# One set of PSUM banks for a small attention, and its last projections moved between the first scores

## The chip, the cores and the metric

The kernel runs on one core of a Trainium2 chip. A core has TensorE (PE in the profile; its weight loads are listed apart as PEld), VectorE (DVE), ScalarE (ACT), GpSimd (POOL) and SyncE (SP), which issues the transfers. Each engine works through its own list of instructions in order and waits on semaphores for the others. Matmul results land in PSUM, which has eight banks of 128 x 512 fp32 values. The metric is the device time of one launch in microseconds, as the median of several runs.

## The reference

The model is a stack of transformer-like blocks on a state `x` of 2 sequences of 256 tokens with 256 features, with a context of 2 x 4096 tokens read by the cross attentions. Each block adds its result to `x`:

```
x = x + L0_xattn(layernorm(x), ctx)      x = x + L0_attn(layernorm(x))   x = x + L0_ffn(layernorm(x))
x = x + L1_xattn(layernorm(x), ctx)      x = x + L1_attn(layernorm(x))   x = x + L1_ffn(layernorm(x))
x = x + L2_xattn(ctx, layernorm(x))      x = x + L2_attn(layernorm(x))   x = x + L2_ffn(layernorm(x))
x = x + L3_xattn(layernorm(x), ctx)      x = x + L3_attn(layernorm(x))   x = x + L3_ffn(layernorm(x))
```

The change concerns two of them, the self attentions of the tokens with 16 heads of 16 features:

```python
def _L1_attn_ref(x, Wq, Wk, Wv, Wu, bu):          # x is the normalized state, 2 x 256 x 256
    q = (einsum('btk,ok->bto', x, Wq) / 4).reshape(b, t, 16, 16)
    kk = (einsum('btk,ok->bto', x, Wk) / 4).reshape(b, t, 16, 16)
    v = einsum('btk,ok->bto', x, Wv).reshape(b, t, 16, 16)
    att = softmax(einsum('bthd,bshd->bhts', q, kk), axis=-1)
    out = einsum('bhts,bshd->bthd', att, v).reshape(b, t, k)
    return einsum('btk,ok->bto', out, Wu) + bu
```

`L3_attn` is the same with one matrix for queries, keys and values, with biases on all of them and on the output, a scale of 1/16, and a band mask: a query sees keys that are at most 128 positions away.

## The kernel before

All blocks are written out one after the other in one program. The state is kept transposed, features on partitions: `x` is 128 x 2 x 512 (two halves of the features, 512 tokens of both sequences). For the two attentions, `small_attention` (L1358) fixes the order of TensorE, VectorE and ScalarE as the program writes it; GpSimd and SyncE are ordered by a scheduler. Before it, the weights are requested by `net.load` in a ring of three buffers.

PSUM is given out by `net.banks`: tiles of one bank in two rings (`mm`, `acc`), and tiles of a pair of banks (128 x 2 x 512) in a ring `sc`. A tile waits until the readers of the tile that had its place before are done. `net.stage` (L97) opens a set with two of each ring, and an SBUF pool `temp` for the pieces of a layer norm.

`small_attention` has three sections.

*Projections*, in a stage of their own. `center` (L223) subtracts the mean of the features and squares (L234, L235). `project` (L1395) then makes, for each of four chunks `c` of 128 padded feature rows (four heads of 32 rows, 16 used), keys and queries of all 512 tokens in one pair of banks `kq_ps`: 2 x 2 matmuls of 128 x 512, each of them two instructions in fp32. After chunk 0, `measure` (L251, L252) has the reciprocal deviation of each token, after chunk 1 `widened` (L271) spreads it over partitions. Then come the values of both pairs of token tiles (`v_ps`, in an `mm` bank), evicted by ScalarE in L1 (L1419) and by VectorE with the bias in L3 (L1422). Then `take` evicts a chunk: VectorE multiplies keys (L1400) and queries (L1404, one per sequence) by the deviation and adds the query bias in L3 (L1406), ScalarE adds the key bias (L1401). With two pairs of banks, chunk 2 reuses the pair of chunk 0, and chunk 3 that of chunk 1.

*Attention*, with another set of banks: `mm` 1, `sc` 3, `acc` 1. There are eight units (sequence, chunk), each with four heads. For a unit, `first_scores` forms the scores of 256 x 256 of four heads in two pairs of banks, by 16 instructions on 32 rows each (L1469), in L3 followed by four bf16 matmuls that add the band (L1477); VectorE takes the negated maximum of each row (L1494, two reductions). `shift_queries` transposes these maxima (L1505) and adds them to the queries as one more feature (L1506), so that the second scores, `scores`, come out shifted and transposed; ScalarE takes their exponential (L1513). `weigh` multiplies with the values (L1524), `inverses` and `normalize` divide. The loop in `attend` runs these staggered: round i transposes the maxima of unit i-1, forms the first scores of unit i, weighs unit i-3, normalizes unit i-4 and forms the second scores of unit i-1. Two scores and two pairs each are four `sc` tiles per round on three pairs of banks, so a tile reuses the place of the third before it.

*Output projection*, in a stage again (`add_projection`, L316).

Of the kernel before, what the change touches and what calls it, by code (L numbers as in the profile page):

```python
# [30 lines left out]
NT = T // P  # L31
# [8 lines left out]
NC16 = H * HP // P  # L40
# [30 lines left out]
class Net:  # L71
# [229 lines left out]
    def project(self, w, chunks, m):  # L301

        ps = self.mm("proj")
        self.matmuls(ps, [(w[:, d, m * P : (m + 1) * P], c) for d, c in enumerate(chunks)])
        return ps
# [294 lines left out]
def run(steps, n=None):  # L600

    for _ in steps if n is None else zip(range(n), steps):
        pass
# [188 lines left out]
class ContextAttention:  # L792
# [46 lines left out]
    def take_queries(self, norm, wq, q_bias, alive):  # L839

        net, nc = self.net, self.nc
        by_batch = lambda ap: ap.rearrange("p (b s) -> p b s", b=NB)
        self.q_bias, self.alive = q_bias, alive
        pair = net.sc("q_ps")
        chunks = net.mm("q_ps"), net.mm("q_ps"), pair[:, 0], pair[:, 1]

        def project(c, copied=True):
            net.matmuls(chunks[c], [(wq[:, d, c * P : (c + 1) * P], of) for d, of in enumerate(norm.chunks)])
            if copied:
                nc.scalar.copy(self.queries[:, :, c], by_batch(chunks[c]))  # L850

        project(0, copied=False)
        net.measure(norm)
        project(1)
        project(2)
        ps = net.widen(norm.rstd)
        nc.scalar.copy(self.wide, ps)
        project(3)
        nc.vector.tensor_tensor(self.q[0], chunks[0][:, :S], self.wide[:, :S], ALU.mult)
        self.add_bias(nc.vector, 0, 0)  # L860
        nc.scalar.copy(self.queries[:, 1, 0], chunks[0][:, S:])
# [145 lines left out]
    def attend(self, vpool, ppool, fpool):  # L1007
        net, nc, PER, LAG = self.net, self.nc, self.PER, self.LAG
        focus = net.focus
        self.vpool, self.ppool = vpool, ppool  # L1010
        for _ in range(4):
            self.load_values_ctx()
        focus.start(self.layer, fpool)
        fills = self.plan()
        n = len(self.UNITS)

        ready = net.sm(1, name="ready", tag="ready")
        nc.scalar.activation(ready, net.eps5, AF.Exp)
        rankings = {}
        for g in range((n + 1) * PER + LAG + 2):  # L1020
            second = g - PER - LAG
            if g < n * PER:
                self.first_scores(g // PER, g % PER)
            run(self.beginning)
            if 1 <= g < n:
                self.finish_queries(g)
            if self.layer == 0:
                for t in self.key_tiles[4:][3 * g : 3 * g + 3]:
                    nc.gpsimd.memset(t, 1.0)
            run(fills.get(g, ()))  # L1030
            for kc in self.rankings.get(g, ()):
                if kc not in rankings:
                    y, _, factor = focus.chunks[kc]
                    rankings[kc] = focus.sparsify(fpool, y, factor)
                run(rankings[kc], 1)
            if 0 <= second < n * PER:
                self.scores(second // PER, second % PER)
            focus.magnitudes_of_taken()
            if 0 <= second - 1 < n * PER:
                self.weigh((second - 1) // PER, (second - 1) % PER)  # L1040
            if g in self.done:
                self.inverses = net.inverses(self.weighed)
                if self.done[g] == n - 1:
                    run(self.normalize(n - 1))
            for kc in self.weighings.get(g, ()):
                run(focus.weighing[kc], 1)
# [311 lines left out]
def small_attention(net, x, wq, wk, wv, wo, scale, qb=None, kb=None, vb=None, ob=None, window=None):  # L1358

    by_program = {mybir.EngineType.PE, mybir.EngineType.DVE, mybir.EngineType.Activation}  # L1360
    with net.tc.manual_schedule(engines=by_program):
        with net.tc.tile_pool(name="sa", bufs=1, reuse_waits="tile") as big, net.tc.tile_pool(name="sa_w", bufs=1, reuse_waits="tile") as work:
            a = SmallAttention(net, big, work, scale, vb, window)
            with net.stage():
                a.project(net.center(net.halves(x)), wq, wk, wv, qb, kb)
            with net.banks(mm=1, sc=3, acc=1):
                a.attend()
            with net.stage():
                return net.add_projection(x, wo, [a.oT[:, c, :] for c in range(NC16)], bias=ob)


class SmallAttention:
# [22 lines left out]
    def project(self, norm, wq, wk, wv, q_bias, k_bias):  # L1395
        net, nc, hc = self.net, self.nc, norm.chunks

        def take(c, k, q):
            of = self.k[:, c, :]
            nc.vector.tensor_tensor(of, k, wide, ALU.mult)  # L1400
            nc.scalar.activation(of, of, AF.Identity, bias=k_bias[:, c : c + 1])  # L1401
            for b in range(NB):
                of, at = self.q[b * NC16 + c], slice(b * S, (b + 1) * S)
                nc.vector.tensor_tensor(of, q[:, at], wide[:, at], ALU.mult)  # L1404
                if q_bias is not None:
                    nc.vector.tensor_scalar_add(of, of, q_bias[:, c : c + 1])  # L1406

        heads = self.v[:, :, : H * VH].rearrange("p t (h e) -> p t h e", e=VH)[:, :, :, :DH]

        def values(t2):  # L1410
            ps = net.mm("v_ps")
            for t in range(2):
                at = slice((t2 + t) * P, (t2 + t + 1) * P)
                net.matmuls(ps[:, t * D : (t + 1) * D], [(c[:, at], wv[:, d, :]) for d, c in enumerate(hc)])
            of = ps.rearrange("p (t h e) -> p t h e", t=2, e=DH)
            for t in range(2):
                rstd = norm.rstd[:, t2 + t : t2 + t + 1]
                if self.v_bias is None:
                    nc.scalar.mul(heads[:, t2 + t], of[:, t], rstd)  # L1419
                else:  # L1420
                    bias = self.v_bias.rearrange("p (h e) -> p h e", e=DH)
                    nc.vector.scalar_tensor_tensor(heads[:, t2 + t], of[:, t], rstd, bias, ALU.mult, ALU.add)  # L1422

        made = []
        for c in range(NC16):
            sc = net.sc("kq_ps")
            for i, w in enumerate((wk, wq)):
                net.matmuls(sc[:, i, :], [(w[:, d, c * P : (c + 1) * P], of) for d, of in enumerate(hc)])
            made.append((c, sc[:, 0, :], sc[:, 1, :]))
            if c == 0:  # L1430
                net.measure(norm)
                continue
            if c == 1:
                wide = net.widened(norm.rstd)
                for t2 in range(0, NT, 2):
                    values(t2)
            for of in made:
                take(*of)
            made = []

    def attend(self):


        n = len(self.UNITS)
        for i in range(n + 4):
            aux = self.net.mm("aux") if 0 <= i - 1 else None
            if 0 <= i - 1 < n:
                self.shift_queries(i - 1, aux[:, S:])
            if i < n:
                self.first_scores(i)  # L1450
            if 0 <= i - 3 < n:
                self.weigh(i - 3)
            if 0 <= i - 4 < n:
                self.normalize(i - 4, aux[:, :S])
            if 0 <= i - 1 < n:
                self.scores(i - 1)
            if 0 <= i - 3 < n:
                self.inverses = self.net.inverses(self.weighed[i - 3], self.acc[:, S:])
# [83 lines left out]
def l1_attn(net, x):  # L1542
    wq, wk = net.load("L1a_wq", "L1a_wk")
    wv, wo = net.load("L1a_wv", "L1a_wo")
    ob, kb = net.vec("L1a_ob"), net.vec("row16")
    return small_attention(net, x, wq, wk, wv, wo, 1.0 / 16.0, kb=kb, ob=ob)
# [446 lines left out]
def l3_attn(net, x):  # L1993
    nc = net.nc
    wq, wk = net.load("L3a_wq", "L3a_wk")
    wv, wo = net.load("L3a_wv", "L3a_wo")
    qb, kb, vb, ob = (net.vec(f"L3a_{n}b") for n in "qkvo")
    return small_attention(
        net, x, wq, wk, wv, wo, D**-0.5, qb=qb, kb=kb, vb=vb, ob=ob, window=P
    )  # L2000
# [363 lines left out]
```

## Time and profile before

| | us |
|---|---|
| median of 3 runs | 2494.8 (2491.27 to 2495.66) |
| profiled execution | 2496.69 |
| its span | 2494.6 |
| L1 attention, first mean matmul after `x` to the next block's | 1611.86 to 1693.72 |
| its projections, first to last chunk | 1614.71 to 1634.84 |
| L3 attention, the same | 2128.87 to 2228.42 |
| its projections | 2132.97 to 2159.45 |
| TensorE busy over the span | 2332.9 |
| VectorE busy | 1532.3 |
| ScalarE busy | 1099.7 |

Times in the profile are microseconds from the start of the span, unless ns is named. A row of the timeline gives start, duration, engine, line, operation, output and inputs, shapes and how many instructions are merged in it; in brackets stands the idle time before it and what ended it. A row of the windows gives the busy time and the number of instructions of each engine in one stretch, then the clock that TensorE was granted as a share of its full speed, the busy share of the transfer engines and GB/s. Line numbers are those of the kernel before.

### The profile page before, as it was taken

Reading aid. Unit: us, or ns where it says so; the run is one execution under the profiler, and the core shown is the slowest. Engines: PE = TensorE matmul, PEld = TensorE weight load, DVE = VectorE, ACT = ScalarE, POOL = GpSimd, SP = SyncE. Lnnn points to the kernel's source line nnn. Section 1 sums busy time; section 2 is a strip of 40 time slices with the busy share of each in tenths; the row PEclk is TensorE's granted clock in tenths of the full one; section 3 lists DMA queues with packets and bytes.
Section 4 is the critical chain, followed back from the end, with each engine's and each line's share of the span. In section 5 each row is a group of like instructions: output and inputs, shape, how many; then the busy total and the mean of one; then the engine's idle time right before and its main releaser. Section 6 shows DMA issues by size and latency. Waiting matters only on the chain.

```text
span 2494.6 us, 42805 instructions
## 1 busy us (share of the span) xinstructions
PE 2332.9 (94%) x17142; PEld 1253.6 (50%) x17142; DVE 1532.3 (61%) x2691; ACT 1099.7 (44%) x1929; POOL 348.2 (14%) x529
## 2 busy tenths in 40 slices
PE   7999999999999699999999999999999986899998
PEld 3454555544544364554454544554448453455453
DVE  4877888788736657877878778443331354334353
ACT  3356555555615334555555565531131352123232
POOL 4000001000024603000010000000011131003020
PEclk9999999999989799999999999989999997788989
DMA  6432233132010124332232231201223100000100
GB/s 196 144 96 91 86 94 92 52 112 65 10 38 35 48 94 127 94 94 87 90 95 86 75 100 29 84 14 51 97 93 93 42 18 14 34 21 12 58 12 22
DMA packets 97798, 174.42 MB, mean 70 GB/s; under 512 B 15120, under 2 KB 63888, under 8 KB 96704
## 3 DMA queue, kind: packets, MB, share of 16 engines
q1 hardware_dynamic: 97600, 171.68, 21.8%
q8 instruction: 136, 2.23, 0.4%
q14 instruction: 62, 0.51, 0.1%
HBM read 154.25 MB, written 0.59 MB: 62 GB/s over the span
## 4 chain that ended last, share of the span: by engine, by line
PE 56%; DVE 5%; ACT 3%; POOL 1%; issue 1%; DMA 0%; ACTq 0%; SPq 0%; DVEq 0%; POOLq 0%
PE s L1149 6%; PE s L1173 5%; PE proj L181 5%; PE attn_acc L1197 5%; PE v_ps L181 4%; PE expert L181 2%; PE k_ps L1070 2%; PE s L181 2%; PE c_acc L1792 2%; PE s L1469 2%; PE ffn_ps L181 2%; DVE mx L1157 2%; PE kq_ps L181 1%; PE f_ps L181 1%; PE kc_sum L181 1%; PE qk_ps L181 1%
## 5 line engine op out<-in xcount | busy, mean ns | idle before, releaser
L1157 DVE TENSOR_REDUCE mx<-s 128x2 f32<-128x1024 f32 x512 | 603.0, 1220 | 229.3 <-PE s L1149 226.6
L1183 ACT ACTIVATE p<-s 128x1024 f32<-128x1024 f32 x512 | 496.0, 1021 | 255.4 <-PE s L1173 253.4
L1173 PE MATMUL s<-xa_q,xa_k 32*128 32x256 f32 x4096 | 342.5, 403 | 25.9 <-DVE mx L1157 23.0
L1149 PE MATMUL s<-xa_k,xa_q 32*128 32x512 f32 x2048 | 337.5, 641 | 5.3 <-ACT p L1183 2.3
L1173 PEld LDWEIGHTS s<-xa_q,xa_k 32*128 32x128 f32 x4096 | 212.8, 184 | 167.7 <-issue 92.6
L1197 PE MATMUL attn_acc<-p,xv 128*32 128x256 f32 x4096 | 276.1, 386 | 0.7 <-ACT p L1183 0.7
L679 DVE TENSOR_TENSOR ge<-fy 128x960 bf16<-128x960 f32 (+14 forms) x240 | 169.5, 706 | 6.5
L1197 PEld LDWEIGHTS attn_acc<-p,xv 128*32 128x32 f32 x4096 | 107.4, 109 | 131.4 <-issue 84.3
L1149 PEld LDWEIGHTS s<-xa_k,xa_q 32*128 32x128 f32 x2048 | 111.3, 183 | 122.6 <-issue 57.5
L633 POOL TENSOR_TENSOR fy<-fy,low 128x256 f32<-128x256 f32 x64 | 46.5, 726 | 866.5 <-ACT fy L632 866.5
L681 DVE TENSOR_TENSOR rank<-rank,ge 128x960 bf16<-128x960 bf16 (+14 forms) x240 | 104.1, 434 | 6.0
L683 DVE TENSOR_TENSOR rank<-rank,ge 128x960 bf16<-128x960 bf16 (+14 forms) x240 | 100.7, 419 | 2.6
L389 POOL TENSOR_SCALAR p<-p,r 128x128 f32<-128x128 f32 (+1 forms) x192 | 83.1, 446 | 128.5 <-DVE r L385 74.5
L1117 ACT COPY xv<-v_ps 128x512 f32<-128x512 f32 x64 | 37.6, 588 | 127.3 <-PE v_ps L181 124.8
L370 ACT ACTIVATE p<-p,top 128x256 f32<-128x256 f32 (+1 forms) x128 | 57.1, 447 | 69.6 <-DVE top L358 68.6
L1070 PE MATMUL k_ps<-ctx_k,w_L0x_wk 128*64 128x512 f32 x256 | 66.8, 616 | 5.3 <-DMA ctx_k<-in_ctxT 5.0
L181 PE MATMUL f_ps<-f_wk,f_ctx 128*128 128x256 f32 x256 | 68.9, 400 | 1.8 <-DMA f_ctx<-in_ctxT 1.8
L181 PEld LDWEIGHTS f_ps<-f_wk,f_ctx 128*128 128x128 f32 x256 | 44.4, 189 | 44.5 <-issue 26.5
L181 PE MATMUL v_ps<-w_L0x_wv,ctx_v 128*128 128x256 f32 x256 | 65.6, 400 | 0.8 <-ACT k_dense L1083 0.8
L1792 PE MATMUL c_acc<-pT,ctx_n 128*128 128x256 f32 x256 | 62.1, 387 | 4.2 <-ACT pT L1765 3.0
L181 PE MATMUL kc_sum<-f_tok,fy 128*128 128x257 f32 x256 | 64.2, 393 | 0.0
L181 PE MATMUL v_ps<-w_L1x_wv,ctx_v 128*128 128x256 f32 x256 | 63.8, 392 | 0.0
(489 smaller groups left out, 3375.7 us busy)
## 6 DMA issues: line engine op xcount, KB each, us to landing
ctx_k<-in_ctxT SPq DMA_DIRECT2D x128, 512.0 KB
ctx_v<-in_ctxT SPq DMA_DIRECT2D x64, 256.0 KB
xa_k<-k_dense SPq DMA_DIRECT2D x512, 32.0 KB
f_ctx<-in_ctxT SPq DMA_DIRECT2D x32, 256.0 KB
f_tok<-in_ctx SPq DMA_DIRECT2D x16, 512.0 KB
ctxT<-in_ctxT SPq DMA_DIRECT2D x16, 512.0 KB
ctx_n<-in_ctx SPq DMA_DIRECT2D x16, 512.0 KB
xa_k<-key_masks SPq DMA_DIRECT2D x128, 8.0 KB
```

The lines of the kernel that those rows point to most:

```text
L181: self.nc.tensor.matmul(out, lhsT=lhsT, rhs=rhs, start=i == 0, stop=i == len(pairs) - 1)
L389: nc.gpsimd.tensor_scalar(p[:, j, :nk], p[:, j, :nk], r[:, j : j + 1], 1.0, ALU.mult, ALU.mult)
L679: nc.vector.tensor_tensor(ge[:, :, :n], w[:, :, :n], w[:, :, P - n :], ALU.is_ge)
L681: nc.vector.tensor_tensor(rank[:, :, P - n :], rank[:, :, P - n :], ge[:, :, :n], ALU.add)
L683: nc.vector.tensor_tensor(rank[:, :, :n], rank[:, :, :n], ge[:, :, :n], ALU.subtract)
L1070: nc.tensor.matmul(ps[i * HR : (i + 1) * HR, :], lhsT=self.wk[:, d, c * HR : (c + 1) * HR], rhs=ctx[:, d, :], start=d == 0, stop=d == ND - 1,)
L1149: nc.tensor.matmul(pairs[i // 2][:, i % 2, :], lhsT=self.q[u][rows, qt * P : (qt + 1) * P], rhs=k[rows, :], start=True, stop=True,)
L1157: nc.vector.tensor_reduce(mx[:, qt, 2 * i : 2 * i + 2, kc], sc, AX.X, ALU.max)
L1173: nc.tensor.matmul(pairs[i // 2][:, i % 2, kk * S : (kk + 1) * S], lhsT=k[rows, at], rhs=self.q[u][rows, :], start=True, stop=True,)
L1183: nc.scalar.activation(p, sc, AF.Exp, scale=DH**-0.5)
L1197: nc.tensor.matmul(self.acc[i * HP : (i + 1) * HP, :S], lhsT=v[:, 2 * k2 + kk, at : at + HP], rhs=ps[i // 2][:, i % 2, kk * S : (kk + 1) * S],
L1792: nc.tensor.matmul(accs[m], lhsT=of[:, (k + i) % (KC // P), m * P : (m + 1) * P], rhs=pT[:, i, :], start=k + i == 0, stop=k + i == KT - 1,)
```

## The change

The projections and the attention share one set of banks (`mm` 1, `sc` 3, `acc` 1), and the `temp` pool stays open through both. `project` becomes a generator, which `attend` drives: its first part makes chunks 0 and 1, the first half of the values, takes chunks 0 and 1, makes chunk 2, the second half of the values, and takes chunk 2; its second part, products and take of chunk 3, runs in the loop right after the first scores of unit 0. No operation is added or dropped. The loop over all values after chunk 1 is split into its two halves, so on ScalarE (L1) and VectorE (L3) the eviction of the second half now stands behind the takes of chunks 0 and 1. On TensorE the order is: chunk 0, variance, chunk 1, widening, values (first half), chunk 2, values (second half), scores of unit 0, chunk 3, transposes of unit 0, scores of unit 1, and so on. On VectorE: take 0, take 1, take 2, reductions of unit 0, take 3, shift of unit 0, reductions of unit 1.

```diff
-            with net.stage():
-                a.project(net.center(net.halves(x)), wq, wk, wv, qb, kb)
-            with net.banks(mm=1, sc=3, acc=1):
-                a.attend()
+            with net.banks(mm=1, sc=3, acc=1), net.tc.tile_pool(name="temp", bufs=2, reuse_waits="tile") as net.temp:
+                a.attend(a.project(net.center(net.halves(x)), wq, wk, wv, qb, kb))
...
-        made = []
-        for c in range(NC16):
+        def products(c):
             sc = net.sc("kq_ps")
             for i, w in enumerate((wk, wq)):
                 net.matmuls(sc[:, i, :], [(w[:, d, c * P : (c + 1) * P], of) for d, of in enumerate(hc)])
-            made.append((c, sc[:, 0, :], sc[:, 1, :]))
-            if c == 0:
-                net.measure(norm)
-                continue
-            if c == 1:
-                wide = net.widened(norm.rstd)
-                for t2 in range(0, NT, 2):
-                    values(t2)
-            for of in made:
-                take(*of)
-            made = []
+            return c, sc[:, 0, :], sc[:, 1, :]
+
+        made = [products(0)]
+        net.measure(norm)
+        made.append(products(1))
+        wide = net.widened(norm.rstd)
+        values(0)
+        take(*made[0])
+        take(*made[1])
+        made = products(2)
+        values(2)
+        take(*made)
+        yield
+        take(*products(3))
+        yield
 
-    def attend(self):
+    def attend(self, projections):
         n = len(self.UNITS)
+        next(projections)
         for i in range(n + 4):
...
             if i < n:
                 self.first_scores(i)
+            next(projections, None)
             if 0 <= i - 3 < n:
                 self.weigh(i - 3)
```

## The prediction

> **What bounds the kernel now.** I read the page first (TensorE 94% busy, 56% of the chain that ended last), then the chain of waits around the two attentions, the timeline of their first 45 us, and last the busy time and granted clock in windows of 3.41 us, because the clock changes only on a grid of that step. The profiled execution took 2496.69 us with a span of 2494.6 us, so 2.1 us lie around the span. The sum is made against it and the forecast is set from the median, 2494.8 us, which is 1.9 us lower.
>
> The timeline of the L1 attention (start, duration, engine, line, operation, idle time before it and what ended that):
>
> ```profile
> 1624.36 3.62 PE L181 MATMUL v_ps<-w_L1a_wv,xc 128*128 128x256 f32 x16
> 1627.81 7.03 PE L181 MATMUL kq_ps<-xc,w_L1a_wq 128*128 128x512 f32 x16
> 1636.38 1.13 PE L1469 MATMUL s<-sa_k,sa_q 32*128 32x256 f32 x12 [0.91 <-DVE sa_q L1404]
> 1637.22 2.36 DVE L1494 TENSOR_REDUCE sa_top<-s 128x4 f32<-128x1024 f32 x2 [0.99 <-PE s L1469]
> 1639.72 0.66 PE L1505 MATMUL aux<-ident,sa_top 128*128 128x128 f32 x2 [2.21 <-DVE sa_top L1494]
> 1645.79 0.69 PE L1505 MATMUL aux<-ident,sa_top 128*128 128x128 f32 x2
> ```
>
> TensorE is fed through the projections (two chunks in 7.03 us, 3.52 each), then waits 0.91 us for VectorE to free a bank pair and 2.21 us for the maxima of the first unit. The first transposes (L1505) open round 1; rounds 2, 3 and 4 open at 1645.79, 1651.82 and 1657.85. Later rounds take 4.8 us. The same places in the L3 attention:
>
> ```profile
> 2147.98 0.88 DVE L1422 SCALAR_TENSOR_TENSOR sa_v<-v_ps,rstd,vectors 128x256 f32<-128x256 f32 x2 [0.85 <-PE v_ps L181]
> 2150.65 8.80 PE L181 MATMUL kq_ps<-xc,w_L3a_wq 128*128 128x512 f32 x16 [2.71 <-DVE sa_q L1404]
> 2165.37 0.66 PE L1505 MATMUL aux<-ident,sa_top 128*128 128x128 f32 x2 [2.32 <-DVE sa_top L1494]
> 2172.61 1.28 ACT L1513 ACT_TABLE_LOAD   x1 [11.67 <-PE s L1477]
> 2172.74 0.64 PE L1505 MATMUL aux<-ident,sa_top 128*128 128x128 f32 x2
> ```
>
> Here chunk 2 starts 2.71 us late, because VectorE evicts all values before it takes chunk 0, and the two chunks take 8.80 us instead of 7.03. Rounds 2, 3 and 4 open at 2172.74, 2181.74 and 2188.45. Windows (length, busy time of PE, PEld, DVE, ACT, POOL with instruction counts, granted clock, DMA):
>
> ```profile
> 1635.74:1639.15 3.41, 1.13 (x12) 0.76 (x12) 2.42 (x4) 1.87 (x2) 0.00 (x0) 1.00 0.74 229
> 1639.15:1642.57 3.42, 2.85 (x20) 2.19 (x22) 0.91 (x3) 0.00 (x0) 0.00 (x0) 0.50 0.01 2
> 1652.81:1656.22 3.41, 3.41 (x32) 1.44 (x28) 1.81 (x3) 0.24 (x1) 0.00 (x0) 0.50 0.00 0
> 2147.73:2151.14 3.41, 0.70 (x2) 0.30 (x2) 3.09 (x8) 0.72 (x1) 0.00 (x0) 1.00 0.00 0
> 2157.97:2161.38 3.41, 2.12 (x10) 0.72 (x8) 2.04 (x6) 0.72 (x1) 0.00 (x0) 1.00 0.23 62
> 2161.38:2164.79 3.41, 1.67 (x16) 1.03 (x16) 2.16 (x3) 0.00 (x0) 0.00 (x0) 1.00 0.62 245
> ```
>
> After a thin window (1.13, 0.70 or 1.67 us busy) the clock is 0.50. In L1 it stays there from 1639.15 to 1656.2, until the weighing of values (L1524) joins; in L3 from 2164.8 to 2185.3. A round then takes 6.03 us in L1.
>
> **The change, L1.** Removed: nothing that computes. Moved: chunk 3 (8 instructions, 3.52 us) goes behind the first score group, and half of the values behind chunk 2. With three bank pairs chunk 2 no longer waits for a bank. TensorE's chain from 1624.36: values 1.81 (half of 3.62), chunk 2 3.52, values 1.81, scores 1.15 (the full-clock groups of 16 at 1661.06), chunk 3 3.52: 1636.17. The first unit's reductions (2.36) run from 1632.7 to 1635.1 under chunk 3, so round 1 opens at 1636.2 instead of 1639.72: 3.5 saved.
>
> Round 1 gets a new wait: VectorE takes chunk 3 (0.69 + 0.74, 1.35 together) before it adds the shift of unit 0. That gives 1637.6 for the take, 1638.05 for the add (0.42) and 1640.45 for two reductions (2.36), which the transposes of round 2 wait for: 1640.55, where it was 1645.79 (5.2 saved). Behind the add queue only the reductions; their waiter is TensorE's second score group, whose second pair of banks frees at 1639.25. At half clock that group's last 12 take 2.08 us (row of 1643.78), so round 2 opens at 1641.4: 4.4 saved. At full clock round 2 lasts 0.35 + 1.5 (score group of 1667.77) + 2.36 + two hand-overs of 0.1 = 4.4, and round 3 at most the steady 4.8: round 4 at 1649.75 instead of 1657.85, 8.1 saved. So L1 gives 4.4 with the clock dropping at once as before, and 8.1 with full clock.
>
> **The change, L3.** VectorE is fuller here: it evicts the values (0.88 for two) and adds the query bias (0.35 each), 2.03 to take a chunk. TensorE from 2144.32: 1.81 + 3.52 + 1.81 + scores and mask 1.6 = 2153.1. VectorE: values to 2147.13, takes to 2149.2 and 2151.2, values to 2152.4, last bank read of chunk 2 at 2154.2. Chunk 3 needs that bank, so TensorE idles 1.1 us and ends chunk 3 at 2157.7; the reductions (2154.45 to 2156.8) are covered. Round 1 opens at 2157.75 instead of 2165.37: 7.6 saved. Of this, 2.7 is the wait for chunk 2's bank and about 1.8 its half clock. Then take 3 to 2159.9, add to 2160.3, reductions to 2162.7, scores and mask to 2163.0: round 2 at 2163.0 (9.7 saved) or, with the late scores at half clock (+1.6), 2164.6 (8.1 saved). Round 2 has the table load (1.28) and Exp (1.02) in its path, since the load waits for the scores as before: 6.3 at full clock against 9.0. Round 3: 5.7 (2188.45 to 2194.07 and on) against 6.7. Full clock throughout saves 13.4.
>
> **Without cost.** The new DMA order is the old one; SP's loads of the first experts wait for chunk 3's weights and go out 1.3 us later than 1634.87, but their first reader runs at 1706.70. GpSimd's list is the same. One bank instead of two for mean, values and transposes: half 2 of the values waits for an eviction that ends at 1627.2 (L1) or 2147.1 (L3), while TensorE gets there at 1629.7 and 2149.65. One accumulator for variance and its widening: the second already needs the first's result. If those covers went, each would cost its eviction, under 0.9 us. From round 1 on every score tile still reuses the tile three before it, so the steady rounds stay.
>
> **The clock.** How much of 4.4 to 8.1 and 8.1 to 13.4 comes depends on it. An estimate from the rows: a full-array instruction of 512 columns takes 3.52/8 = 0.44 us, so a score group (16 instructions of 256 columns on a quarter of the rows) is worth 16 x 0.055 = 0.88 us. The window of 1635.74 with 12 of them has 0.19 of its length and was followed by half clock; that of 2161.38, 12 and four bf16 masks (0.61 us at most, row of 2190.20), 0.19 to 0.37, also; that of 2157.97, with chunk 3 in it, about 0.5, stayed. The new rounds hold two groups: 1.76/4.4 = 0.40 in L1, and in L3 the same with masks over 5.3 to 6.3, but with the table load opening a thin stretch (2163 to 2165.3). That lies between the rows, and where the grid falls decides. I take a drop somewhere in both: L1 6.0 (1.3 of the rounds at 6.03 against 4.4), L3 10.0 (full clock in round 1, then much as before). Sum 16.0: 2496.7 - 16.0 = 2480.7 for the profiled execution, 2478.8 from the median. All full: 21.5, 2473.3. All half: 12.5, 2482.3.
>
> The Trainium skill ("TensorE: Matmul & The Clock Gate", Part 1) says that the clock halves after an idle window of about 3.4 us, and that gaps of over about 3 us are what to avoid. By it the new rounds, with no gap over 2.3 us, would stay at full clock, and the time would be 2473.3. The trace speaks against it: before the drop at 1639.15 the longest gap was 2.21 us. The same page's second failure mode, short idles between bursts through bank cycling, speaks against the change; by it the time is 2482.3.
>
> **Rivals.** (a) The clock stays full in both attentions: 2473.3. For it speaks 0.40 against at most 0.37 where it fell; against it that two or three thin windows in a row must all pass.
> (b) A coarser wait: chunk 3 waits for both reductions of unit 0 and not only for the take of chunk 2. That is 1635.1 instead of 1632.65 in L1 and 2156.8 instead of 2154.2 in L3, 5.1 off the all-half case: gain 7.4, 2487.4. The banks are released tile by tile, which speaks against it.
> (c) Nothing is gained, 2494.8, if the following blocks were held by a load on its own schedule. The loads of the next blocks go out when these blocks end (1693.9, 2228.65), so hardly.
> (d) Slower: the shift moves everything after 1693 on the clock grid. About twelve half-clock stretches follow outside the two attentions; one more window in each costs 1.7 us (half of 3.41), 20.5 in all: 2494.8 - 16.0 + 20.5 = 2499.3. It decides from ten such windows on. The three runs lie within 4.4 us of each other, which bounds such shifts well below that.
>
> **Chances and range.** Forecast 0.55, (a) 0.22, (b) 0.11, (c) 0.04, (d) 0.08. The range goes from all full with 2 us of grid luck (2471) to (b) (2488); outside lies (c), (d) and a little of each. The likeliest case's own range is 2474 to 2483. A difference under 0.2% (5 us) can't be told from none, so faster is 0.88, same 0.04, slower 0.08.
>
> **What would show it.** In the changed profile: chunk 2 starting right behind half of the values without a wait; chunk 3 between the first scores and the first transposes; the L1 transposes about 24.5 us after the L1 mean's first matmul (now 28) and the L3 ones about 29 (now 36.5); the clock rows of rounds 1 to 3. Wrong would be: a wait of TensorE ahead of chunk 3 of over 1.1 us, half clock inside chunk 2 or 3, or steady rounds over 4.8 and 5.7 us.

## The result, and the profile after

The changed kernel takes 2474.44 us in the median of four runs (2471.18 to 2478.97), the kernel before 2494.93 (four runs): the ratio is 0.9916, with a 95% interval of 0.9896 to 0.9936. The profiled execution took 2472.3 us with a span of 2470.5.

The timeline of TensorE in the L1 attention of the changed kernel (columns as in the first fence of the prediction; L1472 is the old L1469, L1508 the old L1505):

```profile
1624.28 1.89 PE L181 MATMUL v_ps<-w_L1a_wv,xc 128*128 128x256 f32 x8
1626.10 1.15 PE L1472 MATMUL s<-sa_k,sa_q 32*128 32x256 f32 x16
1627.17 3.70 PE L181 MATMUL kq_ps<-xc,w_L1a_wq 128*128 128x512 f32 x8
1630.71 0.38 PE L1508 MATMUL aux<-ident,sa_top 128*128 128x128 f32 x2
...
1633.78 1.13 PE L1472 MATMUL s<-sa_q,sa_k 32*128 32x256 f32 x12 [0.43 <-DVE sa_top L1497]
1635.00 0.41 PE L1508 MATMUL aux<-ident,sa_top 128*128 128x128 f32 x2
...
1638.55 2.08 PE L1472 MATMUL s<-sa_q,sa_k 32*128 32x256 f32 x12 [0.47 <-DVE sa_top L1497]
1640.56 0.69 PE L1508 MATMUL aux<-ident,sa_top 128*128 128x128 f32 x2
```

Chunk 3 runs from 1627.17 without a wait, between the first scores and the first transposes, and the 2.21 us for the maxima are gone. Round 1 lasts 4.29 us (1630.71 to 1635.00). The half clock then shows in the durations: twelve scores in 2.08 instead of 1.13 us. The same timeline in L3:

```profile
2135.65 3.60 PE L181 MATMUL kq_ps<-xc,w_L3a_wq 128*128 128x512 f32 x8
2139.08 1.89 PE L181 MATMUL v_ps<-w_L3a_wv,xc 128*128 128x256 f32 x8
...
2143.68 3.67 PE L181 MATMUL kq_ps<-xc,w_L3a_wq 128*128 128x512 f32 x8 [1.09 <-DVE sa_q L1402]
2147.19 0.38 PE L1508 MATMUL aux<-ident,sa_top 128*128 128x128 f32 x2
...
2152.55 0.38 PE L1508 MATMUL aux<-ident,sa_top 128*128 128x128 f32 x2
...
2154.95 1.13 PE L1472 MATMUL s<-sa_k,sa_q 32*128 32x256 f32 x12 [1.39 <-ACT p L1516]
...
2159.24 0.38 PE L1508 MATMUL aux<-ident,sa_top 128*128 128x128 f32 x2
```

Chunk 2 starts right behind half of the values, chunk 3 waits 1.09 us for VectorE, and the scores behind the table load wait 1.39 us for ScalarE. Windows of the changed kernel (columns as in the prediction's windows), four of L1 and three of L3:

```profile
1632.11:1635.52 3.41, 2.41 (x24) 1.37 (x22) 2.82 (x5) 2.49 (x4) 0.00 (x0) 1.00 0.80 222
1635.52:1638.94 3.42, 2.95 (x24) 2.15 (x28) 2.02 (x3) 0.98 (x2) 0.00 (x0) 0.51 0.02 5
...
1642.35:1645.76 3.41, 3.41 (x36) 1.42 (x32) 2.36 (x2) 0.37 (x1) 0.00 (x0) 0.50 0.00 0
1645.76:1649.18 3.42, 3.42 (x46) 2.31 (x42) 1.33 (x3) 1.94 (x2) 0.00 (x0) 0.99 0.00 0
...
2147.51:2150.93 3.42, 2.38 (x25) 1.32 (x24) 3.35 (x8) 0.72 (x1) 0.00 (x0) 1.00 0.74 242
2150.93:2154.34 3.41, 2.52 (x22) 1.55 (x22) 1.61 (x3) 1.75 (x2) 0.00 (x0) 1.00 0.16 65
2154.34:2157.75 3.41, 2.33 (x24) 1.33 (x24) 1.31 (x2) 1.47 (x2) 0.00 (x0) 1.00 0.00 0
```

In L1 the clock falls once, from 1635.52 to 1645.76 (10.2 us, before 17.1). In L3 it stays at 1.00 through all rounds, where before it was halved for 20.5 us.

The comparisons below use marks that are read from the starts of the instructions in each trace. The *block* is the time from an attention's first mean matmul to the next block's. Round openings (the first transposes of each round) are counted from the first value matmul, in us.

| | L1 block | L1 rounds 1, 2, 3, 4 | L3 block | L3 rounds 1, 2, 3, 4 |
|---|---|---|---|---|
| before | 81.86 | 15.36, 21.43, 27.46, 33.49 | 99.55 | 21.05, 28.42, 37.42, 44.13 |
| changed | 76.83 | 11.60, 15.89, 21.45, 27.84 | 87.06 | 13.27, 18.63, 25.32, 31.03 |
| saved | 5.03 | 3.76, 5.54, 6.01, 5.65 | 12.49 | 7.78, 9.79, 12.10, 13.10 |

So the blocks account for 17.5 of the 24.1 us by which the spans differ. From round 4 on the rounds are the same in both kernels (4.75 to 4.82 us in L1, 5.63 to 5.97 in L3). Of the other 6.6, 5.2 lie ahead of the L1 attention, in code that is the same in both (its mean starts at 1606.62 instead of 1611.86). The clock can account for most of the 6.6: over the whole span it is halved for 216.1 us before and 174.9 after; of the difference of 41.3, 30.7 lie in the two attentions and 10.6 elsewhere, and a half-clock stretch costs at most half of its length, here 5.3.

After round 4 each block loses 0.6 us again. TensorE at the end of the L1 attention of the changed kernel:

```profile
1674.32 0.61 PE L181 MATMUL attn_acc<-den,a 128*128 128x4 f32 x4
1675.29 0.64 PE L211 MATMUL aux<-ident,inverses 128*32 128x128 f32 x16 [0.35 <-DVE inverses L203]
1676.47 7.13 PE L181 MATMUL proj<-sa_oT,w_L1a_wv 128*128 128x512 f32 x16 [0.54 <-DVE sa_oT L1542]
```

and of the kernel before:

```profile
1685.21 0.61 PE L181 MATMUL attn_acc<-den,a 128*128 128x4 f32 x4
1686.17 0.64 PE L211 MATMUL aux<-ident,inverses 128*32 128x128 f32 x16 [0.35 <-DVE inverses L203]
1686.75 3.70 PE L181 MATMUL proj<-sa_oT,w_L1a_wv 128*128 128x512 f32 x8
```

Before, the output projection starts without a wait behind the last spreading of the inverses (L211). Now its first instruction waits 0.54 us for the last normalization (L1542 of the changed kernel), which reads that result. From round 8 to the next block's mean it is 17.28 us instead of 16.66 in L1, and 17.62 instead of 17.0 in L3. The prediction did not have this wait.

### The profile page after: what moved, and what is told of

The parts are those of the page before. It is cut to its first block, busy times and chain, and to the rows that moved or that the text cites. A ratio compares the mean times of both kernels' runs of the same rounds, so it can differ in the third digit from the quotient of the medians.

```text
span 2470.5 us, 42804 instructions
## 1 busy us (share of the span) xinstructions
PE 2316.7 (94%) x17142; PEld 1245.2 (50%) x17142; DVE 1532.3 (62%) x2691; ACT 1099.7 (45%) x1929; POOL 348.3 (14%) x529
## 4 chain that ended last, share of the span: by engine, by line
PE 55%; DVE 5%; ACT 3%; POOL 1%; issue 1%; DMA 0%; ACTq 0%; SPq 0%; DVEq 0%; POOLq 0%
PE s L1149 6%; PE s L1173 6%; PE proj L181 5%; PE attn_acc L1197 5%; PE v_ps L181 4%; PE expert L181 2%; PE k_ps L1070 2%; PE s L181 2%; PE c_acc L1795 2%; PE ffn_ps L181 2%; DVE mx L1157 2%; PE s L1472 2%; PE f_ps L181 1%; PE kc_sum L181 1%; PE kq_ps L181 1%; PE qk_ps L181 1%
```

## The experiments

Theory A is the prediction's: the early rounds gain by the order of the work (banks and chunk 3 both), and by a clock that stays up because the windows hold more matmul work. Rival B: the third bank pair with the split values is all, and the place of chunk 3 adds nothing. Rival C: the clock is only a mark of the waits and costs nothing by itself. Rival D concerns versions that move more work: a chunk put between the rounds holds up the second scores behind it. Two later questions are where the 0.6 us at the end come from, and what the table load costs. Where a diff is against the changed kernel, it says so.

### The banks alone (e1)

Chunk 3 goes back ahead of the first scores; the one set of banks and the split values stay. Against the changed kernel:

```diff
         values(2)
         take(*made)
-        yield
         take(*products(3))
         yield
```

> One set of banks and the split values as in the change, but chunk 3 is made and taken ahead of the first scores again. Theory A (the order fills TensorE's gaps, and fuller rounds then keep the clock): the L1 attention gains little here, round 1 (first transposes) opens about 14.5 us after the first value matmul (15.4 before, 11.6 with the change); L3 gains the bank wait of chunk 2 and its half clock, round 1 about 15.3 us after the first value matmul (21.1 before, 13.3 with the change); rounds 1 to 3 as long as before. Time about 2488 (2484 to 2491). Rival B (the third pair of banks is what brings the gain, the place of chunk 3 does not matter): round 1 as early as with the change in both, time 2472 to 2479.

Measured: 2479.41 us, ratio to before 0.9927 (0.9902 to 0.9951). Round 1 opens at 14.29 in L1 and 15.07 in L3, so the banks alone save 1.07 and 5.98 us there, of 3.76 and 7.78. The wait for the maxima is still there, and it is even longer; TensorE in L1 and L3 of this kernel:

```profile
1634.57 0.41 PE L1507 MATMUL aux<-ident,sa_top 128*128 128x128 f32 x2 [2.72 <-DVE sa_top L1496]
...
2150.40 0.41 PE L1507 MATMUL aux<-ident,sa_top 128*128 128x128 f32 x2 [2.96 <-DVE sa_top L1496]
```

Rival B falls by the round openings. The time hardly shows it, because of the clock; it also lies 9 us below theory A's 2488, which had taken rounds 1 to 3 to last as before. In L1 they take 12.4 us together, where it was 18.1. The clock never fell in L1 of this kernel, and the L1 block is 75.62 us, shorter than that of the changed kernel (76.83), though round 1 opens 2.69 us later. The windows around the wait of 2.72 us:

```profile
1630.05:1633.46 3.41, 1.80 (x18) 0.72 (x16) 2.65 (x5) 1.91 (x2) 0.00 (x0) 1.00 0.41 125
1633.46:1636.87 3.41, 1.90 (x22) 1.30 (x22) 2.10 (x3) 0.10 (x1) 0.00 (x0) 1.00 0.33 106
1636.87:1640.29 3.42, 2.76 (x32) 1.98 (x32) 2.18 (x4) 1.94 (x2) 0.00 (x0) 1.00 0.02 5
```

In L3 the clock was halved from 23.8 to 30.6 us after the first value, and the block is 90.24, 3.2 more than in the changed kernel.

### Chunk 3 alone (e5)

The projections keep two pairs of banks and all values together, as before, and only chunk 3 goes behind the first scores. Against the changed kernel:

```diff
-            with net.banks(mm=1, sc=3, acc=1), net.tc.tile_pool(name="temp", bufs=2, reuse_waits="tile") as net.temp:
-                a.attend(a.project(net.center(net.halves(x)), wq, wk, wv, qb, kb))
+            with net.tc.tile_pool(name="temp", bufs=2, reuse_waits="tile") as net.temp:
+                with net.banks():
+                    projections = a.project(net.center(net.halves(x)), wq, wk, wv, qb, kb)
+                    next(projections)
+                with net.banks(mm=1, sc=3, acc=1):
+                    a.attend(projections)
...
         values(0)
+        values(2)
         take(*made[0])
         take(*made[1])
-        made = products(2)
-        values(2)
-        take(*made)
+        take(*products(2))
         yield
         take(*products(3))
```

> Chunk 3 stands between the first scores and the first transposes as in the change, but projections and attention keep their own sets of banks and all values come before the takes, as before. Theory A (order, and the clock that follows from it): in L1 the first scores wait for the take of chunk 2, whose banks they inherit, round 1 opens 12.7 us after the first value matmul (15.4 before, 11.6 with the change); in L3 chunk 2 keeps its wait of 2.7 us, round 1 at about 18.7 (21.1 before, 13.3 with the change). Steady rounds and the output section as before (16.7 and 17.0 us from round 8 to the next block's mean). Time 2484 to 2491, lower where the clock stays full. Rival B (the third pair of banks alone matters): round 1 no earlier than before, time 2493 to 2500.

Measured: 2475.66 us, ratio 0.9918 (0.9898 to 0.9939). Round 1 opens at 12.10 in L1 (3.26 saved) and 17.13 in L3 (3.92 saved). In L3 the old wait ahead of chunk 2 is back, with its half clock; TensorE there:

```profile
2142.40 5.37 PE L181 MATMUL kq_ps<-xc,w_L3a_wq 128*128 128x512 f32 x8 [2.71 <-DVE sa_q L1406]
```

So in L1 chunk 3 is the larger part of what the order saves, in L3 the banks are (5.98 against 3.92). In L1 the parts overlap (1.07 + 3.26 is more than 3.76), in L3 they overlap too (5.98 + 3.92 against 7.78). By time, each part alone lies within the interval of the whole change, and by the blocks it is not far from it: the banks alone save 15.6 us of the 17.5. Chunk 3 alone saves 16.1 (76.71 and 88.61), of which 1.7 are a half-clock stretch ahead of the first value of L3 that stood in the other profiles compared here and not in this one; without them it is 14.4. The two savings overlap, and the second part adds only 2 to 3 us. The time forecast for this kernel, 2484 to 2491, was too high: the rounds open 0.6 and 1.6 us earlier than expected (12.7 and 18.7), and in L3 rounds 1 to 3 keep the full clock.

### The clock by itself: idle matmuls (e2, e3)

The kernel before gets matmuls that use the whole array and whose result nobody reads, behind the first scores of the first three rounds: four of 256 columns in round 0, two in rounds 1 and 2. Nothing else moves:

```diff
             if i < n:
                 self.first_scores(i)
+            if i < 3:
+                self.fill(aux or self.net.mm("aux"), 2 if i else 4)
...
+    def fill(self, ps, n):
+        for _ in range(n):
+            self.net.matmuls(ps[:, :S], [(self.net.ident, self.k[:, 0, :S])])
```

> The kernel before, with idle work for TensorE: four full-array matmuls of 256 columns after the first scores of unit 0 and two each after those of units 1 and 2 (0.44 us each at full clock), whose result nobody reads. Order and banks are those of before. Theory A says the thin windows are what halves the clock: then rounds 1 to 3 run at full clock, together about 13.6 us in L1 (18.1 before) and 17.3 in L3 (23.1 before), and the time is about 2485 (2481 to 2489). Rival C (rounds 1 to 3 are slow because of the chain of maxima and bank releases, the clock is only a mark of idleness): the rounds stay as long or grow by the filling, up to 1.8 us each, time 2495 to 2503.

Measured: 2479.26 us, ratio 0.9921 (0.9893 to 0.9949). TensorE in L1 of this kernel, the windows on the same grid below:

```profile
1638.56 1.15 PE L1476 MATMUL s<-sa_k,sa_q 32*128 32x256 f32 x16
1639.63 1.13 PE L181 MATMUL aux<-sa_k,ident 128*128 128x256 f32 x4
1640.69 1.52 PE L1476 MATMUL s<-sa_q,sa_k 32*128 32x256 f32 x16
1642.31 0.41 PE L1512 MATMUL aux<-ident,sa_top 128*128 128x128 f32 x2
```

```profile
1637.25:1640.66 3.41, 3.12 (x26) 1.85 (x24) 2.10 (x3) 0.00 (x0) 0.00 (x0) 1.00 0.01 4
1640.66:1644.07 3.41, 3.32 (x36) 2.27 (x35) 2.16 (x4) 1.94 (x2) 0.00 (x0) 1.00 0.03 5
```

Work that does nothing shortens the blocks from 81.86 to 76.46 and from 99.55 to 93.52, together by 11.4 us. Round 1 opens where it did (15.37 and 21.06), round 4 at 28.09 instead of 33.49 and at 38.09 instead of 44.13. Rival C falls: the half clock is a cost of its own, and it was 11.4 us of the kernel before in the rounds of these two blocks. The time came out 6 us below theory A's 2485, but the rounds 1 to 3 it rests on take 12.7 and 17.0 us, near the 13.6 and 17.3 that were expected.

The same idle matmuls in rounds 1 and 2 of the changed kernel:

```diff
             next(projections, None)
+            if i in (1, 2):
+                self.fill(aux, 2)
```

> The changed kernel with two such idle matmuls each in rounds 1 and 2, after the first scores. Theory A: the half-clock stretch in the L1 attention goes, rounds 1 to 3 take about 13.6 us there instead of 16.2; L3, at full clock already, stays at 17.8; time 1 to 3 us below the changed kernel, about 2472 (2468 to 2476). Rival C: rounds no shorter, or longer by up to 1.8 us each; 2474 to 2481.

Measured: 2474.82 us, ratio 0.9902 (0.9880 to 0.9923). The L1 half clock is gone, round 4 opens at 24.84 instead of 27.84 and the L1 block is 73.81, 3.0 less. The L3 block is 87.06 as in the changed kernel, where no half clock was left. The median does not show the 3.0 us: its runs lie 9 us apart.

With these two the 17.5 us divide. At full clock in the rounds, the order of the work is worth the difference from e2 to e3: 2.65 in L1 and 6.46 in L3, 9.1. The clock was worth 11.4 before, and 3.0 of it are still lost after: 9.1 + 11.4 - 3.0 = 17.5. The 6.46 still hold one half-clock stretch that belongs to the order: behind the wait of 2.71 us ahead of chunk 2, which e2 keeps, the clock is halved for 3.41 us, at most 1.7 us of cost.

### More work between the rounds (e4)

If a chunk hides the first wait, two might hide more: chunk 2 goes behind the first scores too, chunk 3 into round 1 and the second half of the values into round 2. Against the changed kernel:

```diff
-        made = products(2)
-        values(2)
-        take(*made)
+        yield
+        take(*products(2))
         yield
         take(*products(3))
         yield
+        values(2, net.acc)
+        yield
```

> More is moved behind the first scores: chunk 2 after those of unit 0, chunk 3 after those of unit 1, the second half of the values after those of unit 2 (in the accumulator bank). Theory A: round 1 opens about 8.2 us after the first value matmul in L1 (11.6 with the change), round 4 about 2 to 4 us earlier than with the change in each attention, all at full clock, since rounds 1 and 2 get full-array work; time about 2468 (2464 to 2473). Rival D (the first scores then wait for the biased keys, and chunk 3 holds up the second scores of round 1): what is saved ahead of round 1 is lost within it, time 2473 to 2480.

Measured: 2476.39 us, ratio 0.9903 (0.9878 to 0.9928). Round 1 opens at 8.09 (L1) and 10.15 (L3), 3.51 and 3.12 earlier than in the changed kernel. Round 3 opens at 21.40 and 26.28, where it was 21.45 and 25.32: everything is given back, in L1 even though its clock never falls here. The time lies in rival D's range and not in theory A's. Rival D is right in part, as round 1 now lasts 6.38 and 7.22 us instead of 4.29 and 5.36. The other part is in round 2; ScalarE and TensorE of this kernel there, in L1:

```profile
1633.39 1.28 ACT L1517 ACT_TABLE_LOAD   x1
...
1634.68 1.94 ACT L1517 ACTIVATE p<-s 128x1024 f32<-128x1024 f32 x2
...
1635.76 1.13 PE L1473 MATMUL s<-sa_k,sa_q 32*128 32x256 f32 x12 [1.64 <-ACT p L1517]
```

The table load now stands between the second scores and the bank pair that the next first scores need. Round 2 lasts 6.93 us in L1 and 8.91 in L3, and in L3 the clock falls in it.

### The table load and the last bank (e6)

Two edits on the changed kernel. An Exp of a constant, whose result nobody reads, runs on ScalarE behind the first scores of unit 0, so that the table is there before it is needed. And the mean takes its bank from `acc`. A ring gets its banks in the order in which the rings are first used: in the kernel before the attention's set begins with `sc`, in the changed one with the mean's `mm`, so that `aux` and with it the last normalization sit in the first bank, which the output projection's first tile inherits. (This is read from the program and the waits; no trace shows the places of the tiles.)

```diff
-        mean = self.mm("mean")
+        mean = (bank or self.mm)("mean")
...
-                a.attend(a.project(net.center(net.halves(x)), wq, wk, wv, qb, kb))
+                a.attend(a.project(net.center(net.halves(x), bank=net.acc), wq, wk, wv, qb, kb))
...
+            if i == 0:
+                early = self.work.tile([P, 1], F32, name="early", tag="early")
+                self.nc.scalar.activation(early, self.net.eps5, AF.Exp)
             next(projections, None)
```

> The changed kernel, with one Exp of 128 x 1 on ScalarE in round 0, so that its table is there before the second scores, and the mean of the layer norm in the accumulator bank, so that the output projection does not inherit the bank of the last normalization. If the table load in L3's round 2 and the bank of the output projection are what the chain shows: round 2 of L3 5.4 us (6.7 with the change), from round 8 to the next mean 16.7 us in L1 and 17.0 in L3 (17.3 and 17.6 with the change, 16.7 and 17.0 before), in all 2.5 us less, about 2472. Rival: the key bias of chunk 3 after the early Exp reloads a table, or the projection waits for the last unit's output anyway: no gain, 2474 to 2477.

Measured: 2473.49 us, ratio 0.9910 (0.9881 to 0.9940), which can't be told from the changed kernel. The blocks can: 76.21 and 83.19. From round 8 to the next mean it is 16.66 and 17.0 us, as before the change. That it is the bank and not the early Exp, kernels without either edit show (L1): 17.27 or 17.28 in e1, e3 and e4, which begin their set with the mean, and 16.65 in e5, whose attention has its own set. Round 2 of L3 lasts 5.40 instead of 6.68 us; ScalarE of the changed kernel and then of this one:

```profile
2152.58 1.28 ACT L1516 ACT_TABLE_LOAD   x1 [3.74 <-PE s L1480]
2153.87 1.94 ACT L1516 ACTIVATE p<-s 128x1024 f32<-128x1024 f32 x2
```

```profile
2154.34 1.94 ACT L1519 ACTIVATE p<-s 128x1024 f32<-128x1024 f32 x2 [3.76 <-PE s L1483]
```

The load is 1.28 us and the round gets 1.28 shorter. The Trainium skill ("ScalarE: Activation LUTs", What ACT_TABLE_LOAD costs) gives 1283 ns for the load, which agrees, and a drain of some 1.38 us beside it for each switch; here the Exp starts 0.01 us behind the load, ScalarE had been idle for 3.74 us ahead of it, and the saving shows no such drain. Of the L3 block's 3.9 us, 1.3 are this load, 0.6 the bank and 0.3 a later round (5.97 to 5.69, its cause is open); 1.7 are a half-clock stretch ahead of the first value that this execution did not have.

### Both, with idle matmuls (e7), and with the spread (e8)

e7 is e3 with the two edits of e6, e8 is e4 with them.

> The changed kernel with the idle matmuls in rounds 1 and 2, the early Exp and the mean in the accumulator bank together. If the three add up: L1 from its mean to the next block's 73.2 us, L3 85.2, time about 2471 (2467 to 2475). Rival: with the Exp earlier the idle matmuls stand in the way of the second scores of round 2, up to 0.9 us lost in each attention: 74.1 and 86.1, time about 2473.

> The kernel with chunks 2 and 3 and half of the values spread over rounds 0 to 2, with the early Exp and the mean in the accumulator bank. If its long round 2 (6.9 us in L1, 8.9 in L3) comes from the table load and the Exp behind it, as its chain shows: round 2 of 5.2 in L1 and about 6.5 in L3, L1 from mean to mean 72.9 us, L3 83.3, time about 2470 (2465 to 2474). Rival: the second scores, held up by chunk 3 in round 1, set round 2 in any case: rounds no shorter, time about 2475.

Measured: e7 2468.64 us, ratio 0.9891 (0.9858 to 0.9924), blocks 73.20 and 84.89, so the three add up as forecast; e8 2463.40, below the forecast range of 2465 to 2474, ratio 0.9877 (0.9851 to 0.9904), blocks 73.13 and 82.50, with full clock in all rounds. In e8 round 2 lasts 5.50 us in L1 and 5.98 in L3, instead of 6.93 and 8.91: what e4 lost in round 2 was the table load and, in L3, the clock that fell behind it. The rows of e8 that answer to those of e4:

```profile
1633.40 1.92 ACT L1520 ACTIVATE p<-s 128x1024 f32<-128x1024 f32 x2
...
1634.45 1.13 PE L1476 MATMUL s<-sa_k,sa_q 32*128 32x256 f32 x12 [0.21 <-ACT p L1520]
```

The scores wait 0.21 us for ScalarE and not 1.64. Rounds 1 of 6.38 and 7.22 us stay, as a chunk still stands ahead of the second scores; 2.1 and 1.9 us of what the earlier opening saves are lost there.

### The change and the best version, once more (r1, r2)

> The changed kernel once more, unaltered, to see what of a profile repeats. Order theory: from the first value matmul to round 1 11.6 us in L1 and 13.3 in L3 again, to 0.05 us; the steady rounds 4.82 and 5.69; output sections 17.3 and 17.6. Clock theory: the place of the half-clock stretches, and so the length of rounds 2 and 3 (L1 4.3 to 6.4 us each) and of the work ahead of the first attention (1605.9 to 1617.9 us in the profiles so far, with the same code) differ from execution to execution. Time 2472 to 2478, ratio about 0.991.

> The kernel with chunks 2 and 3 and half of the values in rounds 0 to 2, the early Exp and the mean in the accumulator bank, once more with more rounds. L1 73.1 and L3 82.5 us from mean to mean at full clock, up to 1.7 more in L3 where its prefix starts in a half-clock stretch. 8 us below the changed kernel on the same chip (5 to 11), ratio to the kernel before about 0.988. Rival: the low median of its first timing was luck of the clock, ratio as the changed kernel's, 0.991.

Measured, on one chip: the change 2475.93 us in six runs, ratio 0.9915 (0.9896 to 0.9933); e8's kernel 2468.23 us in four (2467.92 to 2472.77), ratio 0.9889 (0.9867 to 0.9912). Both are faster than before. That e8's kernel is faster than the change rests on the blocks more than on the times, whose intervals overlap: the two blocks together are 163.89 and 163.87 us in the two profiles of the change, 155.63 and 155.62 in the two of e8's kernel, 8.3 us less. Not all of it is earned: 1.7 of the 8.3 are a half-clock stretch ahead of the first value of L3, in code that is the same. It stood in both profiles of the change and in neither of e8's kernel (from the first mean matmul to the first value 15.4 us against 13.7). From the first value on the gain is 6.6.

## Why the prediction was right, step by step

**L1, the order.** Forecast: round 1 opens 3.5 us earlier, round 2 5.2 at full clock (4.4 at half). Measured 3.76 and 5.54, with the clock full until 0.5 us after round 2 opened. The chain through take 3, the shift and the reductions is the one named: VectorE took chunk 3 from 1630.91, added the shift at 1632.18 and ended the reductions at 1634.86, and round 2 opened at 1635.00. Chunk 3 did not wait at all, so rival (b), a coarser wait, is refuted.

**L3, the order.** Forecast: round 1 7.6 and round 2 9.7 earlier, with 1.1 us of wait ahead of chunk 3. Measured 7.78, 9.79 and 1.09. The split named there (2.7 for the wait of chunk 2, 1.8 for its half clock) is roughly borne out by e5, where both are back: round 1 opens 3.86 us later than in the change. The two make 4.5, and chunk 3 waits 0.78 us less there (0.31 against 1.09), which leaves 3.7.

**The clock.** Forecast: a drop somewhere in both, L1 6.0 and L3 10.0. Measured at round 4: 5.65 and 13.10. L1 came close in part by luck: at full clock it gains 8.65 us (e3) where 8.1 were forecast, and the drop takes 3.0 of it where 2.1 were allowed. In L3 the step that failed is "L3 10.0 (full clock in round 1, then much as before)": no window fell, and the gain is the full-clock value of 13.4 almost whole. The full-clock sums themselves held in both.

The estimate of the load of a window did better than the assumption that was put on it. It counts 0.055 us for a score instruction. By the same measure two full-array transposes of 128 columns are 0.11 each, a quarter of 0.44. The last window ahead of the L1 drop (1632.11) has some 18 scores and the two transposes, 1.2 of 3.41 us or 0.36; it was followed by half clock. The window of 1633.46 in e1 has 20 scores and two transposes, 1.3 us or 0.39, and stayed. The clock's grid lies alike in both (0.17 and 0.14 of a step at the first value), so here the load makes the difference and not the phase.

For L3 the masks count, and the trace has their weight: bf16 matmuls of 256 columns start 0.109 us apart, the fp32 ones of the values 0.216. With 0.11 us for a mask, and the work cut at the ends of each window, the estimate sorts all 551 windows in the two blocks of the twelve profiles. Full clock fell after 18 of them, at 0.13 to 0.37, and stayed after 497, at 0.39 or more; half clock stayed after 18, at 0.37 or less, and ended after 18, at 0.41 or more. So the prediction's bounds of 0.37 and 0.40 were right. In L3 it took a drop for the thin stretch at the table load; that stretch (the wait of 1.39 us up to 2154.95) lies across the end of a window, and the two windows that share it have 0.45 and 0.40.

Over the whole program the estimate needs the share of the array's columns as well as of its rows, and it sorts less cleanly. All 242 falls lie at 0.39 or below, but full clock also stayed after 37 of 7835 windows below 0.38, 17 of them in the first 13 us. It remains an estimate, its bounds are read from these traces, and no run varied the load of one window alone.

What decides is not the gap. The Trainium skill ("TensorE: Matmul & The Clock Gate", Part 1) lets the clock fall after an idle window of about 3.4 us. Here it fell after a window of the changed kernel whose longest gap was 0.48 us and which was busy for 2.41, and it stayed up in e1 through a gap of 2.72 us and two windows busy for 1.80 and 1.90. The grid of 3.41 us agrees with the page; a rule by gaps or by busy time alone does not fit these windows.

**Without cost.** One bank for mean, values and transposes cost nothing within the attention, and the steady rounds stayed as forecast. The step that failed is the same sentence read further: that only the two evictions hang on the bank. The order of first use decides which bank the output projection inherits, and it cost 0.6 us in each block.

**The sum.** 16.0 us were forecast for the blocks and 17.5 came: 3.1 more from L3 (13.1 for 10.0), 0.35 less from L1 (5.65 for 6.0) and 1.2 less for the two waits at the end: 16.0 + 3.1 - 0.35 - 1.2 = 17.5. The median fell by 20.5, 3 more than the blocks. These 3 lie in code that is the same in both, and within what executions of one kernel differ by. So the time came 4.4 us below the forecast, inside the range and inside the likeliest case's own. The blocks lie between that case and rival (a), all full (21.5), and nearer to the first; the median lies nearer to (a)'s 2473.3 only by those 3 us. Rival (c), no gain, falls with the time. Rival (d) would have added half clock outside the two attentions; there it is 171.8 us before and 161.2 after. But 181.7 in the second profile of the change (r1) shows that this part moves by 20 us between executions of one kernel.

## What to carry to other kernels

Where TensorE is fed by short matmuls on few rows, as in these rounds, a wait can cost twice, by itself and by the half clock behind it. Filling the wait with full-array work that must be done anyway pays for the wait. It pays for the clock only where the windows behind it stay loaded too: in L1 chunk 3 was done before the thin window came, and the block took 76.83 us, against 75.62 with the banks alone; spread over the rounds, with the table load out of the way (e8), such work kept the full clock. Read single steps by marks inside the block (round openings, the next block's start), since a step of 3 us is exact there and invisible in a median of runs 5 to 10 us apart. When sets of banks are merged, look also at what the next set inherits, and move a table load off the path before moving more work into the rounds.

## What was not expected of the hardware

The two profiles of the changed kernel have the same blocks (163.89 and 163.87 us) and spans of 2470.5 and 2481.5. The granted clock is halved for 174.9 us in the one and 195.3 in the other; half of this difference, 10.2, would be nearly all of the 11.0. Over the twelve profiles the L1 attention begins anywhere from 1605.9 to 1617.9 us, though the code ahead of it is the same.

The clock's grid lies at any place against the start of the span (from 0.03 to 0.97 of a step over twelve profiles, worked out from the starts of half-clock stretches). At the first value of L3 it lies within 0.87 to 1.03 of a step in all twelve, and at that of L1 within 0.14 to 0.20 in nine and 0.66 to 0.78 in three. So the drops in the rounds repeat from run to run (in L1 from 16.5 us after the first value in one profile of the change and 16.4 in the other), where the clock theory of r1 expected them to move. The kernel before is one of the three at the other phase of L1, so how much of its half clock there belongs to the phase isn't shown. Why the program falls into step with the grid is open.
